# Quantized experts: tokens in tiles of four, the shared gate in halves, and two of three roundings on GpSimd

## The chip, the cores and the metric

The kernel runs on one core of one Trainium2 chip. A core has five engines that work side by side, each through its own instructions in a fixed order: TensorE (PE in the profile; PEld is its weight load), VectorE (DVE), ScalarE (ACT), GpSimd (POOL) and SyncE (SP), which here only issues DMAs. An instruction waits at the head of its engine's order until the semaphores that it names have been raised, and everything behind it on that engine waits with it. The metric is the time of one execution on the device in microseconds (us), less being better; the median of three runs is given, and one further execution was recorded by the profiler.

## The reference

The whole program is two decoder layers with six sublayers, each followed by a residual sum and a layer norm. The change lies in the first sublayer, a mixture of experts with quantized ("bit") linear layers. Cut to what matters:

```python
def bitlinear(x, w):
    xn = rmsnorm(x, BIT_EPS)
    xq = activation_quant(xn)      # round(x * 127 / max|x|), then scaled back
    wq = weight_quant(w)           # clip(round(w / mean|w|), -1, 1) * mean|w|
    return xq @ wq.T

def bit_mlp(x, gate_proj_w, down_proj_w):
    gate, y = split(bitlinear(x, gate_proj_w), 2)
    return bitlinear(silu(gate) * y, down_proj_w)
```

Each of 2048 tokens (16 blocks of 128, 256 numbers per token) goes through one shared expert and through the best two of eight routed experts, each of which takes 320 tokens at most. An expert's gate matrix is 256 x 1024 and its down matrix 512 x 256. To quantize a matrix one needs the mean of the absolute values of all of it; to quantize a token, or a row of the inner layer, one needs that row's largest absolute value and its sum of squares.

## The kernel before, in words

The sublayer is the function stage0 (L119 to L729). The order of every engine's work is written out by hand: no scheduler moves anything, and the order of the calls in the source is the order on each engine.

SP first issues the loads (L156 to L172): eight blocks of tokens as eight DMAs, the shared expert's gate (1 MB) and down matrix (0.5 MB), the other eight blocks, small tables, the transposed tokens xT for the router, the first routed expert's matrices, the context and more.

The head (L589 to L628) prepares the shared expert. For each block of tokens, squared (L266) sums squares on ACT, measured (L263) finds the largest value on DVE, steps (L273) makes the scale and quantized (L282) rounds the block with two DVE instructions; normed (L277) has POOL make the block's factor. For the weights, sum_down (L225) and sum_gate (L231) add up absolute values, total (L233) adds over the partitions with a matmul by ones on PE, means (L237) makes the scale, up (L242) scales and rounds on ACT by adding a large constant, and low and high (L246, L249) take the constant off again and clip, on DVE.

Then follows a loop of 36 turns (L689 to L729), one for each tile of 128 rows: 14 tiles of the shared expert, 20 of the routed experts, and two more shared ones. The turns overlap. In turn n, in the order of the source: ACT turns the earlier tile's transposed rows into bf16 (turned, L550); DVE multiplies the two halves of the inner layer (hidden, L516); ACT computes silu for the tile after (L511); DVE finds the row maximum (largest, L524), ACT the squares (L520), DVE the step and its reciprocal (step_of, L529 and L530) and the rounded inner rows m_r (rounded, L541); DVE (or ACT) scales the result of tile n-2 (done, L564 to L570); PE computes a bank of keys or values for a later stage (L1945, L1952), the gate of tile n+2 (gated, L503) and the down product of tile n-1 (down, L557); POOL makes the factor of tile n-1 (factor, L535: m_rt, m_rs, m_s); DVE or ACT copies the bank out (out_of, L585; from turn 11 on DVE does it in two turns of three, and not where n leaves 1 when divided by 3). Then come the jobs listed for the turn: quantizing the weights of the next routed experts (made_in, L636: the last DVE instructions of an expert fall in turns where n leaves 1), the router (logits L296, turn_logits L306, routes L314), copies of factors (backs_of, L454) and gathers of token rows by indirect DMA (fetch, L444) on POOL. Last, PE transposes the rounded rows (turn, L546).

The PSUM tile that down writes has one buffer, so down(n-1) waits until done(n-2) has read it. The tiles that the transposes write have two buffers, which the router's transposed logits share: while routes has not read those (L321), a later transpose waits.

After the loop the next stage begins with the gather of the routed results.

## Time and profile before

| what | value |
|---|---|
| median of three runs | 1404.76 us (1403.98 to 1405.64) |
| profiled execution | 1408.86 us, span from first to last instruction 1407.2 us |
| busy over the span | PE 88%, DVE 59%, ACT 48%, POOL 35% |
| mean granted TensorE clock | 0.954 of full speed |
| first tile: hidden(0) starts | 23.58 us |
| hidden(3), hidden(4), hidden(5) start | 39.71, 51.02, 58.64 us |
| last tile: hidden(35) starts | 191.35 us |
| first matmul of the next stage | 199.13 us |

The share of a whole span says little about a stage, so the sublayer has to be read in stretches of its own. A row of the table of stretches gives the length of the stretch, then for PE, PEld, DVE, ACT and POOL the busy time in us and the number of instructions, then the granted clock, the share of time in which the DMA engines moved data, and GB/s. A row of the timeline gives start, length, engine, line, operation, what is written and read with shapes, and in brackets how long the engine had been idle before and what released it. A row of the chain of waits gives start and length of a piece of the chain that ended last.

### The profile page before, as it was taken

Reading aid. Unit: us, or ns where it says so; the run is one execution under the profiler, and the core shown is the slowest. Engines: PE = TensorE matmul, PEld = TensorE weight load, DVE = VectorE, ACT = ScalarE, POOL = GpSimd, SP = SyncE. Lnnn points to the kernel's source line nnn. Section 1 sums busy time; section 2 is a strip of 40 time slices with the busy share of each in tenths; the row PEclk is TensorE's granted clock in tenths of the full one; section 3 lists DMA queues with packets and bytes.
Section 4 is the critical chain, followed back from the end, with each engine's and each line's share of the span. In section 5 each row is a group of like instructions: output and inputs, shape, how many; then the busy total and the mean of one; then the engine's idle time right before and its main releaser. Section 6 shows DMA issues by size and latency. Waiting matters only on the chain.

```text
span 1407.2 us, 19229 instructions
## 1 busy us (share of the span) xinstructions
PE 1234.8 (88%) x6731; PEld 843.2 (60%) x6743; DVE 824.7 (59%) x1755; ACT 676.4 (48%) x1733; POOL 495.5 (35%) x669
## 2 busy tenths in 40 slices
PE   4678887889978899866998999999889999999995
PEld 1455444666654566643655788877777655666553
DVE  7799968989957887856244565667333111211115
ACT  5779865778956665544223566654522111111110
POOL 4256547668861776640043233222202000000003
PEclk9899989989999999987899999999999999999998
DMA  8358324110011211100100222211005222232002
GB/s 311 131 174 295 114 79 85 17 39 31 32 50 60 74 51 46 53 16 24 52 0 1 73 78 62 75 61 45 1 8 187 71 98 68 78 105 96 17 8 75
DMA packets 63120, 103.53 MB, mean 74 GB/s; under 512 B 11920, under 2 KB 41712, under 8 KB 62768
## 3 DMA queue, kind: packets, MB, share of 16 engines
q1 hardware_dynamic: 60848, 96.76, 20.6%
q0 software_dynamic: 2176, 5.55, 1.9%
q8 instruction: 53, 0.87, 0.3%
q14 instruction: 43, 0.35, 0.1%
HBM read 81.74 MB, written 16.35 MB: 70 GB/s over the span
## 4 chain that ended last, share of the span: by engine, by line
PE 52%; DVE 29%; ACT 8%; POOL 6%; issue 4%; DMA 1%; another core or an unknown queue 0%; SPq 0%; DVEq 0%; ACTq 0%; POOLq 0%
PE ps_y L2453 7%; PE ps_m L2442 7%; PE ps_g L2442 7%; PE ps_m L1998 4%; DVE acc L1306 2%; PE ps_m L2129 2%; ACT s L2100 2%; PE ps_t L2120 2%; PE ps_m L2018 2%; DVE cT L1315 1%; DVE s L915 1%; DVE m L2094 1%; DVE s L2090 1%; PE ps_t L2109 1%; PE ps_s L2087 1%
## 5 line engine op out<-in xcount | busy, mean ns | idle before, releaser
L82 POOL TENSOR_SCALAR ln_t<-ln_mv 128x1 f32<-128x1 f32 (+1 forms) x84 | 16.6, 197 | 450.7 <-DVE ln_mv L90 309.1
L2447 DVE TENSOR_TENSOR h<-h,ps_m 128x512 f32<-128x512 f32 x60 | 41.3, 688 | 228.3 <-PE ps_m L2442 228.3
L2100 ACT ACTIVATE s<-s,m 128x128 f32<-128x128 f32 x256 | 99.4, 390 | 69.1 <-DVE m L2094 69.1
L2446 ACT ACTIVATE h<-ps_g 128x512 f32<-128x512 f32 x60 | 35.8, 597 | 171.0 <-PE ps_g L2442 171.0
L2442 PE MATMUL ps_g<-xin,w 128*128 128x512 f32 x224 | 106.3, 592 | 0.0
L2442 PE MATMUL ps_m<-xin,w 128*128 128x512 f32 x224 | 105.3, 592 | 0.0
L2453 PE MATMUL ps_y<-w,h 128*128 128x256 f32 x448 | 97.8, 379 | 0.0
L2453 PEld LDWEIGHTS ps_y<-w,h 128*128 128x128 f32 x448 | 85.1, 190 | 14.6 <-issue 3.3
L2104 POOL TENSOR_TENSOR s<-s,t 128x1024 f32<-128x1024 f32 x32 | 60.7, 1898 | 90.7 <-DVE t L2103 90.7
L927 ACT ACTIVATE s<-s,m 128x128 f32<-128x128 f32 x256 | 83.3, 395 | 11.7 <-DVE m L922 11.7
L2442 PEld LDWEIGHTS ps_m<-xin,w 128*128 128x128 f32 x224 | 42.5, 190 | 51.4 <-issue 50.2
L2442 PEld LDWEIGHTS ps_g<-xin,w 128*128 128x128 f32 x224 | 42.0, 190 | 46.4 <-issue 45.0
L1998 PE MATMUL ps_m<-xT,half 128*128 128x256 f32 x256 | 62.6, 389 | 2.6 <-DVE qT L2003 1.9
L2454 ACT COPY y<-ps_y 128x256 f32<-128x256 f32 x30 | 11.2, 372 | 104.7 <-PE ps_y L2453 67.7
L2090 DVE TENSOR_TENSOR s<-ps_s,hide 128x1024 f32<-128x1024 f32 x32 | 39.2, 1224 | 35.9 <-PE ps_s L2087 35.9
L2129 PE MATMUL ps_m<-half,oT 128*128 128x256 f32 x256 | 59.3, 385 | 0.0
L1306 DVE SCALAR_TENSOR_TENSOR acc<-ps_m,l1a_conv_w,acc 128x508 f32<-128x508 f32 (+2 forms) x72 | 53.3, 740 | 3.5 <-ACT acc L1299 1.8
L1998 PEld LDWEIGHTS ps_m<-xT,half 128*128 128x128 f32 x256 | 47.4, 194 | 9.2 <-DVE qT L2003 2.3
L2129 PEld LDWEIGHTS ps_m<-half,oT 128*128 128x128 f32 x256 | 47.4, 190 | 7.5
L83 POOL TENSOR_TENSOR ln_rs<-ln_t,mhalf 128x1 f32<-128x1 f32 (+1 forms) x84 | 48.7, 579 | 7.0
L2100 ACT ACTIVATION_READ_ACCUMULATOR s<-s,m 128x1 f32 x256 | 48.2, 188 | 0.0
L1414 POOL TENSOR_TENSOR mT<-mT,bc 128x1024 f32<-128x1024 f32 x16 | 37.8, 2360 | 28.4 <-ACT mT L1396 16.3
(524 smaller groups left out, 3102.1 us busy)
## 6 DMA issues: line engine op xcount, KB each, us to landing
w<-in_w_gate_dram SPq DMA_DIRECT2D x9, 1024.0 KB
csb<-cs_dram SPq DMA_DIRECT2D x16, 512.0 KB
w<-in_l1f_gateT_dram SPq DMA_DIRECT2D x14, 512.0 KB
w<-in_l1f_upT_dram SPq DMA_DIRECT2D x14, 512.0 KB
w<-in_l1f_downT_dram SPq DMA_DIRECT2D x14, 512.0 KB
k<-kv SPq DMA_DIRECT2D x20, 256.0 KB
v<-kv SPq DMA_DIRECT2D x20, 256.0 KB
ring<-k SPq DMA_DIRECT2D x10, 512.0 KB
```

Of the source, the lines that this page charges most:

```text
L83: return self.nc.gpsimd.tensor_tensor(out, t, self.mhalf[: out.shape[0], :n], ALU.pow)
L927: nc.scalar.activation(at, at, AF.Exp, bias=m[h][:, i:i + 1])
L1306: nc.vector.scalar_tensor_tensor(accv[:, :, j:], pcv[:, :, :P - j], w.conv[:, c, TAPS - 1 - j:TAPS - j], accv[:, :, j:], ALU.mult, ALU.add,)
L1414: nc.gpsimd.tensor_tensor(st[n].mT, st[n].mT, bc, ALU.mult)
L1998: nc.tensor.matmul(pq[:, j, :], wt[k][:, at], src[:, k, :], start=(k == 0), stop=(k == KD - 1))
L2090: nc.vector.tensor_tensor(half(b, j), pss.rearrange("p r c k -> p (r c) k"), hide.unsqueeze(1).to_broadcast([P, 8, P]), ALU.add,)
L2100: nc.scalar.activation(at, at, AF.Exp, bias=m[j][:, i:i + 1], accum_out=t[j][:, i:i + 1])
L2104: nc.gpsimd.tensor_tensor(half(b, j), half(b, j), t[j].unsqueeze(2).to_broadcast([P, 8, P]), ALU.mult)
L2129: nc.tensor.matmul(py[b], oT[b][:, c, :], w.o[c // 4][:, c % 4, :], start=(c == 0), stop=(c == NC - 1))
L2442: nc.tensor.matmul(ps[:, j, :], m[k][:, c * P:(c + 1) * P], self.r.xin[:, k, e, cols], start=(k == 0), stop=(k == KD - 1),)
L2447: nc.vector.tensor_tensor(h, h, pu, ALU.mult)
L2453: nc.tensor.matmul(pd, rows(c), w.down[c // 4][:, c % 4, :], start=(c == 0), stop=(c == FI // P - 1))
```

## The change

1. Loads. The tokens lie in four tiles of four blocks and come in four DMAs in place of sixteen. The shared gate comes in two halves of 0.5 MB right behind the first four blocks; the down matrix comes behind the second four.
2. The head. The shared expert has its own function, first_weights. Of the gate's absolute sums, ACT does one half and DVE the other; the gate is scaled, rounded and clipped half by half; the down matrix follows on its own, with a matmul for its mean of its own. Blocks 8 to 11 are measured, and blocks 12 to 15 squared, in turn 0; the quantizing of blocks 8 to 11 moves one turn later, and blocks 12 to 15 are all quantized in turn 3. POOL's factor for the router (rs_gate) is made in turn 1 in place of turn 0.
3. The loop. In turns where n does not leave 0 when divided by 3 (24 of 36), rounded runs on POOL. It stands in POOL's order ahead of the factor of tile n-1 and of the turn's jobs.
4. The gathers: two to a turn in place of three.

Behind the loop the order on every engine is as it was.

```diff
-        self.x = [self.new(self.const, [P, D], F32, f"x{b}") for b in range(NB)]
+        self.xs = [self.new(self.const, [P, 4, D], F32, f"x{g}") for g in range(NB // 4)]
+        self.x = [self.xs[b // 4][:, b % 4, :] for b in range(NB)]
...
-        for b in range(NB // 2):
-            nc.sync.dma_start(x[b], K.ins["x"][b])
-        load(NE)
-        for b in range(NB // 2, NB):
-            nc.sync.dma_start(x[b], K.ins["x"][b])
+        def load_tokens(g):
+            nc.sync.dma_start(K.xs[g], K.ins["x"][4 * g:4 * g + 4].rearrange("b p d -> p b d"))
+
+        load_tokens(0)
+        w = raw[NE] = K.new(wp, [P, 3, 4 * D], F32, "w")
+        for k in range(KD):
+            nc.sync.dma_start(w[:, k, :], K.ins["w_gate"][NE][k * P:(k + 1) * P, :])
+        load_tokens(1)
+        nc.sync.dma_start(
+            w[:, 2, :].rearrange("p (k n) -> p k n", n=D), K.ins["w_down"][NE].rearrange("(k p) n -> p k n", p=P),
+        )
+        load_tokens(2)
+        load_tokens(3)
...
+        def first_weights():
...
+            def sums():
+                nc.scalar.activation(q[:, 0, :], w[:, 0, :], AF.Abs, accum_out=acc[:, 0:1])
+                nc.vector.tensor_reduce(acc[:, 1:2], w[:, 1, :], AX.X, ALU.add, apply_absolute_value=True)
+
+            def mean(i):
+                pt = K.new(ps, [P, 1], F32, "ps_o", bufs=1)
+                at = (0, 1) if i == 0 else (2,)
+                for j in at:
+                    nc.tensor.matmul(pt, K.ones, acc[:, j:j + 1], start=(j == at[0]), stop=(j == at[-1]))
+                nc.vector.tensor_scalar(
+                    back[:, i:i + 1], pt, 1.0 / (D * 2 * FF) if i == 0 else 1.0 / (D * FF), 1e-5, ALU.mult, ALU.max,
+                )
+                nc.vector.reciprocal(s[:, i:i + 1], back[:, i:i + 1])
+
+            def up(k):
+                nc.scalar.activation(w[:, k, :], w[:, k, :], AF.Identity, scale=s[:, k // KD:k // KD + 1], bias=magic)
+
+            def whole(k):
+                to = q[:, k, :] if k < KD else qd[:, 0, :]
+                nc.vector.tensor_scalar(to, w[:, k, :], MAGIC, 1.0, ALU.subtract, ALU.min)
+                nc.vector.tensor_scalar(to, to, -1.0, None, ALU.max)
+
+            def sum_down():
+                nc.vector.tensor_reduce(acc[:, 2:3], w[:, 2, :], AX.X, ALU.add, apply_absolute_value=True)
...
         def rounded(n):
             g, t = tiles[n]
             r[n] = K.new(work, [P, FF], F32, "m_r", bufs=2)
-            nc.vector.tensor_scalar(r[n], h[n], g.s2[:, t:t + 1], MAGIC, ALU.mult, ALU.add)
+            on = nc.gpsimd if n % 3 else nc.vector
+            on.tensor_scalar(r[n], h[n], g.s2[:, t:t + 1], MAGIC, ALU.mult, ALU.add)
...
+        w = first_weights()
+        for b in range(2):
             quantized(b)
         normed(0)
-        w = weights(NE)
+        w.sums()
+        quantized(2)
+        w.mean(0)
+        quantized(3)
+        w.up(0)
         prepare(groups[0])
         tokens(groups[0], 0)()
+        w.whole(0)
+        scaled(groups[0])
+        w.up(1)
+        w.whole(1)
+        for b in range(4, 8):
+            squared(b)
+        w.sum_down()
+        gated(0)
+        silu(0)
+        w.mean(1)
+        w.up(2)
+        gated(1)
         for b in range(4, 8):
             measured(b)
+        w.whole(2)
         steps(1)
         normed(1)
...
+        for b in range(8, 12):
+            job(0, measured, b)
+        job(0, steps, 2)
+        job(0, normed, 2)
+        for b in range(12, 16):
+            job(0, squared, b)
+        job(1, lambda: K.rsqrt(small, rs_gate, ss, 1.0 / D, 1e-6, "rs_t"))
...
-            job((b - 8) // 2, quantized, b)
+            job(1 + (b - 8) // 2, quantized, b)
...
-            job(2 + (b - 12) // 2, quantized, b)
+            job(3, quantized, b)
...
-                job(m + t // 3, fetch, j, range(t, t + 1))
+                job(m + t // 2, fetch, j, range(t, t + 1))
```

## The prediction, made blind

> **What bounds the kernel now.** I read the stretches first. Behind the routed experts nothing changes, so only the first 199.1 us matter.
>
> ```profile
> core 0: us, PE busy (x) PEld busy (x) DVE busy (x) ACT busy (x) POOL busy (x), PEclk, DMA share, GB/s
> 58.64:100.00 41.36, 31.72 (x200) 22.77 (x203) 38.20 (x101) 32.60 (x52) 19.85 (x34) 0.96 0.41 132
> 100.00:140.00 40.00, 34.07 (x197) 23.49 (x200) 37.60 (x83) 35.78 (x59) 24.71 (x53) 1.00 0.87 283
> 140.00:163.30 23.30, 20.08 (x107) 10.67 (x105) 22.12 (x52) 20.21 (x32) 14.72 (x30) 1.00 0.39 132
> 163.30:183.60 20.30, 19.49 (x108) 10.77 (x109) 18.91 (x42) 13.38 (x27) 7.30 (x17) 1.00 0.31 114
> ```
>
> DVE is 92 to 95% busy from turn 5 (58.64) to 163.3; ACT follows with up to 89%. From 163.3 on PE is 96% busy. The chain of waits says the same: one DVE piece after another in the middle, PE at the end.
>
> ```profile
> 106.90 0.67 DVE m_h L516
> 107.59 0.70 DVE m_am L524
> 109.10 0.48 DVE x L564
> 109.58 0.60 DVE kv L585
> 110.18 1.12 DVE w_acc L225
> ...
> 176.42 1.72 PE ps_k L1952 x4
> ```
>
> So DVE time taken out of turns 5 to 26 shortens the run, and out of turns 27 to 33 it does not. The timeline shows how much goes with one rounding:
>
> ```profile
> 108.50 0.17 DVE L530 RECIPROCAL m_s<-m_st 128x1 f32<-128x1 f32 x1
> 108.70 0.49 DVE L541 TENSOR_SCALAR m_r<-m_h,m_s 128x512 f32<-128x512 f32 x1
> 109.10 0.48 DVE L564 SCALAR_TENSOR_TENSOR x<-ps_o,m_s,x 128x256 f32<-128x256 f32 x1
> ```
>
> The row is 0.49 long, but the next starts 0.40 after it: a rounding occupies DVE for 0.40.
>
> The early turns are bound by single waits:
>
> ```profile
> 13.24 1.22 DVE L225 TENSOR_REDUCE w_acc<-w 128x1 f32<-128x1024 f32 x1 [2.31 <-DMA w<-in_w_down_dram]
> ...
> 25.31 2.90 POOL L83 TENSOR_TENSOR rs_gate<-rs_t,mhalf 128x16 f32<-128x16 f32 x1
> ...
> 36.80 0.66 PE L546 MATMUL ps_t<-ident,m_r 128*128 128x128 f32 x4 [2.03 <-DVE pr L321]
> ...
> 39.71 0.75 DVE L516 SCALAR_TENSOR_TENSOR m_h<-ps_y,m_s,m_sg 128x512 f32<-128x512 f32 x1 [2.24 <-ACT m_sg L511]
> ```
>
> DVE waits for the shared weights; turn(1) waits until the router's logits are read (pr, 36.46), and hidden(3) hangs on that through turned(1), the tokens' copy and silu(3).
>
> The groups give prices, and a late stage shows what two engines do to each other:
>
> ```profile
> L541 DVE TENSOR_SCALAR m_r<-m_h,m_s 128x512 f32<-128x512 f32 x36 | 17.7, 492 | 1.8
> L1614 POOL TENSOR_SCALAR l1a_out_proj<-l1a_out_proj,l1a_ssm_norm_w 128x256 f32<-128x256 f32 x4 | 1.9, 484 | 0.0
> ```
>
> ```profile
> 402.28 0.73 POOL L989 TENSOR_TENSOR r<-x,bo_all 128x256 f32<-128x256 f32 x1
> 402.35 0.81 DVE L1003 TENSOR_SCALAR x<-r,ln_mv,ln_rs 128x256 f32<-128x256 f32 x1 [0.36 <-POOL ln_rs L83]
> ```
>
> L1003 takes 0.40 where POOL is idle (386.16). Here it lasts until 0.15 after POOL's end: DVE was held, and of its own 0.40 it had 0.25 behind it. The reductions (L524) and the reads of PSUM (L564, L585) show no such stretching.
>
> **The change, part by part.** *Loads.* Tokens land now 0.66 apart ((5.44 - 2.80)/4, blocks 0 to 4); SP stalls on them from 5.55 to 13.56. In one DMA four blocks land at 2.80 + 0.39 MB at 199 to 373 GB/s (slowest and fastest early rate), so 3.9 to 4.8: I take 4.3, against 4.7 for the fourth block now. Each 0.5 MB behind it takes 1.4 at 373 GB/s: gate halves 5.7 and 7.1, blocks 4 to 7 8.5, down 9.9, where now the gate lands at 11.74 and down at 13.24. SP's remaining loads start some 4 us earlier; none is waited for in the loop. Seven DMAs in place of eighteen save SP issue time that nothing waits for later; the store of the quantized tokens (turn 3) goes out 1.2 later, its first gather is in turn 8.
>
> *Head.* DVE in its new order: measured 0 to 3, 1.5 (5.8); steps (6.2); two blocks quantized, 0.6 each (7.4); half the gate summed 1.22 (8.65); identity cast and third block (9.5); mean (9.9); fourth block (10.5). ACT's up(0) takes 1.25 (L244, half size) to 11.2, whole(0) 0.69 + 0.43 to 12.4. ACT copies xqT (1.0) before up(1), so whole(1) ends at 14.6; down's sum 15.9; PE's gate matmuls hold its mean back to 16.85; measured 4 to 7 18.3; whole(2), behind silu's table load and up(2), 19.8; steps and four blocks 22.6. hidden(0) then starts at 22.6 instead of 23.58: -1.0, and not the 4 us by which the weights come sooner, because DVE took on half the gate's sum (+1.22) and now waits for ACT in small pieces. Measuring blocks 8 to 11 (1.4 + 0.4) falls to turn 0 and quantizing two (1.2) leaves it: hidden(1) at 27.05 (-0.3).
>
> *Turns 1 to 4.* Turn 1 without its rounding: hidden(2) -0.6. POOL's queue then holds m_r(1), the factor of tile 0 (1.25), rs_gate (0.2 + 2.9) and only then normed(3) and m_r(2). rs_gate ends at about 35.4, where it ended at 28.2; L321 now waits for it and starts at 35.55, against 36.46: hidden(3) -0.9. The four quantized blocks in turn 3 fill DVE's wait for the router's exp (1.1 now). m_r(2) comes at 38, still ahead of its transpose (41.67 - 0.9). In turn 4 the rounding's 0.40 goes: hidden(5) -1.3. If rs_gate comes 0.9 later, this falls to -0.4; if the tokens land at 3.9 it is -1.7.
>
> *Rounding on POOL.* No row has POOL on this form. L82 with one element takes 0.19, L1614 with 256 0.484; straight on, 512 elements give 0.77. Upper end: two-input POOL rows of 512 elements, 1.28 (L935). I take 0.77: same operation, one input. DVE to POOL takes 0.14 (22.69 to 22.83). With the reciprocal's end as zero, POOL works from 0.14 to 0.91, while DVE runs done from 0.03 to 0.46. Next on DVE:
> - n leaves 2 from turn 8 on (8, 11, 14, 17, 20, 23, 26): a PSUM read or copy, then a reduction. Nothing is held; -0.40 each, -2.8.
> - n leaves 1 (7, 10 to 25 by threes) and turn 5: L247 or L390, operations of the held kind (a two-input one: L750 takes 3.82 for two of 0.48 at 270.06, beside POOL's sums). By the row above they end 0.91 - 0.25 after zero plus their length, 0.20 later than free: -0.20 each, eight times -1.6.
>
> Turns 1 and 2 hold nothing: in 1 DVE's quantizing is first, in 2 POOL comes late. m_r is ready for PE at 0.97, when down(n-1) (now released 0.40 sooner by done) ends: turn(n) is not late. Behind m_r on POOL waits the factor of tile n-1, ready at 2.2; done(n-1) needs it a turn (4.2) later. In the last turns PE transposes at 195.61 what was rounded by 193.80; 0.4 more is hidden there.
>
> *POOL's queue.* After turns 13, 19 and 25 it is: m_r 0.77, factor 1.25, eight copies of 0.22, two gathers of 1.12 (one in 25) and gaps 0.3: 6.3 (5.1) against turns of 4.2 to 4.6. The next m_r comes 1.7 (0.6) late, turn(n) 1.3 (0.2) later than now; PE's waits for done of 0.5 to 1.0 hide about half: +1.5. Spreading the gathers costs nothing else: POOL idles 63 us waiting for squares.
>
> *ACT and PE close behind* (89%, 86%) take back a tenth of 4.4: +0.4. From 163.3 on 0: PE bounds.
>
> Sum: -1.3 - 2.8 - 1.6 + 1.5 + 0.4 = -3.8. The profiled execution, 1408.86 with span 1407.2 and 1.66 around it, becomes 1405.1; it lies 4.1 above the median 1404.76, so in the median's terms 1401.0.
>
> The Trainium skill, SBUF — State Buffer, section Who interferes with whom, speaks against the change: DVE's two-port and two-input operations and GpSimd exclude each other, and "the other fully blocks" for the whole instruction. The rows above agree that it blocks, but credit 0.25 already done. Without that credit the eight held turns would gain nothing (0.45 of waiting against 0.40), and the sum would be -1.8.
>
> **The rivals.** *Slower: POOL's rounding is dear.* If 512 elements with two operations cost 1.5, the eight held turns lose 1.5 - 0.57 - 0.40 = 0.53 each (+4.2), the free ones keep 0.2 (-1.4), the head keeps -0.3, POOL's queue costs 1.5: 1408.8. It decides above about 1.35. For it: 1.28 for two inputs; against: L1614.
>
> *Nothing measurable: other waits take it.* rs_gate late by 0.9 (-0.4 in the head), ACT and PE take half of 4.4, queue +0.3: about -1.5, 1403.3. For it: ACT's 89% at 100 to 140, and the chain's excursions to PE at 82 to 89, 114 and 141.
>
> *Much faster: no holding.* All fifteen turns give 0.40 (-6.0), head -2.0 with early tokens: -8, 1396.8. For it: weights four us sooner; against: L1003.
>
> **How the numbers follow.** Chances: forecast 0.40, no change 0.24, much faster 0.20, slower 0.16. A measurement here tells about 0.2%, 2.8 us. The forecast's own range is 1398.5 to 1403, so a quarter of it counts as same; of the no-change case a sixth as faster; of the slower case nearly all as slower. Faster 0.54, same 0.31, slower 0.15. The range reaches through most of the outer cases: 1395.5 to 1408.5.
>
> **What the profile after would show.** Right: m_r on POOL at about 0.77; hidden(0) near 22.6 and hidden(5) near 57.3; L247 stretched by 0.2 or more in turns that leave 1; the next stage's first matmul near 195.3. Wrong: m_r above 1.3, POOL's waits ending in long DVE runs with turn(n) waiting for m_r, or hidden(0) below 21, which would mean that DVE did not bound the head.

## The result, and the profile after

The changed kernel takes 1406.63 us (median of 12 runs; without one of them, which took 2089.76 us at a granted clock of 0.554 and is left out of the ratio, the median is 1405.45 and the range 1402.59 to 1414.17); the kernel before took 1405.31 us (12 runs beside them, 1400.49 to 1410.56). The ratio is 1.0008, with a 95% interval of 0.9990 to 1.0026: no difference that can be told. The profiled execution took 1414.17 us (span 1412.3, mean granted clock 0.947), 5.3 more than the profiled execution of before.

Line numbers of the changed kernel are higher: hidden is L559, the row maximum L567, the step and reciprocal L572 and L573, the rounding L585, POOL's factor L83, L84 and L579, the transposes L590, done L608 and L614, the copied bank L629, the weights' low and high L255 and L258, gathers L492, copies of scales L503 to L506.

The stretches of the profile after, from hidden(5) on, with cuts at 100 and 140 as before, at hidden(27) and at hidden(33) (columns as there):

```profile
core 0: us, PE busy (x) PEld busy (x) DVE busy (x) ACT busy (x) POOL busy (x), PEclk, DMA share, GB/s
56.50:100.00 43.50, 33.40 (x209) 23.87 (x210) 40.25 (x101) 35.09 (x57) 23.97 (x42) 0.92 0.45 145
100.00:140.00 40.00, 33.30 (x193) 22.54 (x196) 36.13 (x76) 34.27 (x54) 30.23 (x58) 1.00 0.88 281
140.00:161.30 21.30, 18.89 (x100) 10.13 (x98) 19.58 (x44) 19.16 (x32) 15.18 (x30) 1.00 0.31 104
161.30:184.65 23.35, 20.80 (x115) 11.14 (x114) 17.63 (x40) 15.21 (x31) 12.71 (x27) 1.00 0.30 105
```

DVE has fallen from 94 to 90% between 100 and 140 and from 95 to 92% behind it. The last row should not be set against the 96% of before, whose cuts lay elsewhere: from hidden(27) to hidden(33) PE was busy for 19.79 of 21.81 us before, 91%, against 89% now. Work has left DVE, but the tiles don't come faster by as much: somebody waits. What the roundings cost on POOL, and who waited for them, stands in the view of the tile m_r:

```profile
L585 POOL TENSOR_SCALAR m_r<-m_h,m_s x24: 677/687/1672, 28.8 to 192.0; 128x512 f32<-128x512 f32 x24
...
who waited for it (us, times):
  ACT m_hT L594: 27.9, 21
  PEld ps_t L590: 9.8, 7
  PE ps_t L590: 8.0, 6
```

The rounding takes 0.69 in the median (shortest, median, longest in ns), but up to 1.67, and PE sat 8.0 us waiting for it, where before it never did. Since each turn starts with its hidden(n) on DVE, the starts of hidden(n) tell where time went. The table adds up by how much the turns differ from the first profile of before (negative: shorter; turn n runs from hidden(n) to hidden(n+1)):

| turns | forecast | after |
|---|---|---|
| up to hidden(5) | -1.3 | -2.14 |
| 8, 11, ... 26 (n leaves 2) | -2.8 | -3.31 |
| 7, 10, ... 25 (n leaves 1), with turn 5 | -1.6 | +1.31 |
| behind POOL's queue: 21 and 27 | +1.5 | +1.71 and +1.48 |
| all others up to hidden(28) | | -0.08 |
| hidden(28) | | -1.03 |
| hidden(28) to hidden(35) | 0 | -0.41 |
| hidden(35) to the next stage's first matmul | 0 | +0.47 |
| sum: next stage's first matmul | -3.8, with +0.4 for ACT and PE | -0.97 (198.16) |

### The profile page after: what moved, and what is told of

Its sections match the earlier page's. It is cut to its first block, busy times and chain, and to the rows that moved or that the text cites. A ratio compares the mean times of both kernels' runs of the same rounds, so it can differ in the third digit from the quotient of the medians.

```text
span 1412.3 us, 19212 instructions
## 1 busy us (share of the span) xinstructions
PE 1245.6 (88%) x6735; PEld 851.8 (60%) x6747; DVE 823.9 (58%) x1735; ACT 674.7 (48%) x1734; POOL 512.1 (36%) x693
## 4 chain that ended last, share of the span: by engine, by line
PE 54%; DVE 23%; ACT 8%; POOL 8%; issue 4%; DMA 2%; another core or an unknown queue 0%; SPq 0%; POOLq 0%; DVEq 0%; ACTq 0%
PE ps_y L2501 7%; PE ps_m L2490 7%; PE ps_g L2490 7%; PE ps_m L2046 4%; ACT s L2148 2%; DVE acc L1354 2%; PE ps_t L2168 2%; PE ps_m L2177 2%; PE ps_m L2066 2%; DVE m L2142 1%; DVE s L2138 1%; DVE cT L1363 1%; DVE s L963 1%; PE ps_s L956 1%; PE ps_t L998 1%
## 5 line engine op out<-in xcount | busy, mean ns | idle before, releaser
L83 POOL TENSOR_SCALAR ln_t<-ln_mv 128x1 f32<-128x1 f32 (+1 forms) x84 | 16.3, 194 | 457.7 <-DVE ln_mv L91 308.5
L84 POOL TENSOR_TENSOR ln_rs<-ln_t,mhalf 128x1 f32<-128x1 f32 (+1 forms) x84 | 48.5, 577 | 7.0
```

The costliest lines, as they stand in the source:

```text
L84: return self.nc.gpsimd.tensor_tensor(out, t, self.mhalf[: out.shape[0], :n], ALU.pow)
```

## The experiments

In the diffs here "-" is the changed kernel unless another is named. A free turn is one where n leaves 2, a held turn one where n leaves 1. "Next stage" is the start of the next stage's first matmul, the end of the sublayer that the change touches.

**The kernel before, profiled again.** No edit.

> The kernel before, unchanged, profiled once more, to see how far hidden(n) moves with nothing changed. In the kernel with the old head and roundings on GpSimd hidden(0) came at 22.89 against 23.58 in the first profile, with the same code up to there. Theory A (the weights' landing scatters): hidden(0) between 22.6 and 23.6, the turns from 5 to 14 and 16 to 34 as long as in the first profile to within 0.1, turn 15 and the stretch from hidden(35) to the next stage's first matmul off by up to 1.5. Rival (the stage repeats to within 0.2 everywhere): hidden(0) at 23.6 and the next stage at 199.1.

hidden(0) came at 22.57 in place of 23.58, hidden(5) at 58.06 (-0.58), turn 15 was 0.51 shorter, the last stretch 0.56 shorter, the next stage began at 197.63 in place of 199.13. All turns from 8 to 14 and 16 to 34 were the same within 0.03. Theory A. So with the order of work unchanged a turn's length can be compared to a few hundredths (turn 7, which moved by 0.18, and turn 15 excepted), but the head, turn 15 and the last stretch move by half a microsecond to one without any change; and the whole execution took 1397.53 us, 11.3 less than the first profiled one.

**The head alone.**

```diff
-            on = nc.gpsimd if n % 3 else nc.vector
+            on = nc.vector
```

> The changed kernel with all 36 roundings back on VectorE; the loads, the split shared weights, the turns 0 to 4 and the gathers' places stay as changed. Theory A (the head gives about 2, the roundings on GpSimd give nothing in sum): hidden(5) starts 1.7 before the 58.64 of the kernel before (2.14 in the changed kernel, less the 0.4 of turn 4's rounding), the turns from 6 to 26 take what they took before to within 0.1, and the next stage's first matmul is at 197.6 (199.13 before, 198.16 changed). Theory B (whatever VectorE gains early is taken back by ScalarE and TensorE before the stage ends): next stage at 198.8 to 199.2. Total: A about 1.5 us below before (ratio 0.999), B 1.000.

hidden(5) at 57.70: 0.94 before the first profile, 0.36 before the second. From turn 6 on the turns took what they took before within 0.24, but for turn 15 (-1.21). Next stage 196.53, ratio 0.9976 (0.9959 to 0.9993). Theory A for what follows the head, though with up to 0.24 in place of its 0.1; but the head gave half of what A said, and turn 15 and the last stretch (-0.88), two of the places that scatter, brought the next stage forward instead. Of the changed kernel's 2.14, 1.33 fall in turn 4, which is as long as before here, with its rounding back on DVE.

**The roundings alone**, on the kernel before:

```diff
-            nc.vector.tensor_scalar(r[n], h[n], g.s2[:, t:t + 1], MAGIC, ALU.mult, ALU.add)
+            on = nc.gpsimd if n % 3 else nc.vector
+            on.tensor_scalar(r[n], h[n], g.s2[:, t:t + 1], MAGIC, ALU.mult, ALU.add)
...
-                job(m + t // 3, fetch, j, range(t, t + 1))
+                job(m + t // 2, fetch, j, range(t, t + 1))
```

> The kernel before with only the roundings of two turns in three moved to GpSimd and the gathers two to a turn; loads and head as before. Theory A: turns that leave 2 are 0.4 to 0.5 shorter each, turns that leave 1 are 0.2 longer each, turns 21 and 27 are 1.5 to 1.7 longer because the rounding of turn 20 and 26 stands behind copies and gathers in GpSimd's queue; next stage at 199.9 to 200.5, total ratio 1.0005 to 1.001. Rival (the prediction's prices: -0.2 in each turn that leaves 1 and +1.5 for the queue in all): next stage at 196.3.

The turns behave as in the changed kernel: those that leave 2 give -3.05, those that leave 1 cost +1.42, turns 21 and 27 cost +1.71 and +1.48, just as there. hidden(28) is 0.19 before the first profile and 0.75 behind the second. The next stage, at 196.83, was not as late as A said, because the last stretch took 1.7 less, one of the places that scatter. Ratio 0.9977 (0.9966 to 0.9987). So within the turns more is lost from turn 7 on than the free turns give; A's total is not borne out, and the rival's 196.3, though near in the sum, is wrong in each of its terms.

**A third of the roundings, in free turns.**

```diff
-            on = nc.gpsimd if n % 3 else nc.vector
+            on = nc.gpsimd if n % 3 == 2 else nc.vector
```

> The changed kernel with GpSimd rounding only in the turns that leave 2 (12 of 36), where VectorE has no two-port run behind its reciprocal. Theory A (the loss sits in the turns that leave 1): each of the turns 8, 11, 14, 17, 23 gives 0.45, the turns that leave 1 are as long as before, turns 20 and 26 still lose 0.7 to 1 behind copies and gathers; hidden(28) 3 before the old one, next stage at 196.0 to 197.0, total ratio 0.998. Rival (the loss sits in GpSimd's queue alone): next stage at 198, as in the changed kernel.

The turns that leave 2 gave -3.43; those that leave 1 cost 0.67 where the changed kernel lost 1.38, nearly all of it in turn 7 (0.19, which scatters) and in turn 22 (0.43, of which more below); turn 21 cost 0.04. But turn 27 cost 4.49, turn 15 1.03, and the next stage came at 200.09; ratio 0.9987 (0.9966 to 1.0009). The timeline shows what happened to the rounding of turn 26:

```profile
161.61 0.18 POOL L506 COPY m_b<-w_back 64x1 f32<-64x1 f32 x1 [1.55 <-issue]
...
162.81 1.06 POOL L492 DMA_INDIRECT xe<-xq_dram,token  x1 [0.29 <-POOL m_b L506]
...
163.97 0.70 POOL L585 TENSOR_SCALAR m_r<-m_h,m_s 128x512 f32<-128x512 f32 x1
164.72 1.05 PE L590 MATMUL ps_t<-ident,m_r 128*128 128x128 f32 x4 [2.56 <-POOL m_r L585]
```

POOL stood still for 1.55 among the copies for no reason that the trace names; the copies and a gather stood ahead of the rounding; PE waited 2.56 for it, and its four transposes then took 1.05, where those of the turn ahead took 0.60. The granted clock from 158 to 171 was 0.87 (1.00 in the kernel with the head alone). Theory A is right on the turns that leave 2 and on those that leave 1 but for turn 22; turn 27 it undercounted.

**A third of the roundings, in held turns.**

```diff
-            on = nc.gpsimd if n % 3 else nc.vector
+            on = nc.gpsimd if n % 3 == 1 else nc.vector
```

> The changed kernel with GpSimd rounding only in the turns that leave 1 (12 of 36), where the low and high halves of the expert's weights follow on VectorE. Theory A: each of the turns 7 to 25 that leave 1 ends 0.2 to 0.3 later than with all on VectorE, GpSimd's rounding takes 1.0 to 1.7 there, hidden(27) at about 0 to -0.5 against before, next stage at 198.6 to 199.3, total ratio 1.000. Rival (the prediction's -0.2 for each such turn): next stage at 196.2 and ratio 0.998.

The turns that leave 1 are 1.01 longer in sum, 0.8 more than with the head alone; hidden(27) is 1.14 before the first profile, so 0.6 later than with the head alone; POOL's rounding took 1.24 to 1.73 in five of seven such turns. But turn 22 alone is 1.04 longer, and that ahead of its reciprocal, where DVE waited 1.51 for PE (0.35 before). Turn 16 cost 0.31, turn 10 0.11, and turns 7, 13, 19 and 25 are 0.10 to 0.12 shorter each. The next stage, 196.85, and the ratio, 0.9976 (0.9960 to 0.9991), are better than A said: the head, turn 15 (-1.22) and the last stretch (-0.74) were short. Neither A's loss of 0.2 to 0.3 in each such turn is there nor the rival's gain of 0.2: a held turn gives about 0.1 or loses up to 0.3.

**Where the time of a held turn goes.** The trace of the changed kernel has both orders of arrival. The timeline of DVE and POOL in turns 13 and 19:

```profile
101.54 0.17 DVE L573 RECIPROCAL m_s<-m_st 128x1 f32<-128x1 f32 x1
101.62 0.47 DVE L608 SCALAR_TENSOR_TENSOR x<-ps_o,m_s,x 128x256 f32<-128x256 f32 x1
101.87 0.69 POOL L585 TENSOR_SCALAR m_r<-m_h,m_s 128x512 f32<-128x512 f32 x1 [5.27 <-DVE m_s L573]
102.00 1.10 DVE L255 TENSOR_SCALAR q_d<-w 128x1024 bf16<-128x1024 f32 x1
...
128.41 0.67 DVE L255 TENSOR_SCALAR q_d<-w 128x1024 bf16<-128x1024 f32 x1
128.68 1.49 POOL L585 TENSOR_SCALAR m_r<-m_h,m_s 128x512 f32<-128x512 f32 x1 [1.46 <-DVE m_s L573]
129.00 0.69 DVE L258 TENSOR_SCALAR q<-q 128x2048 bf16<-128x2048 bf16 x1
129.61 0.84 DVE L258 TENSOR_SCALAR q_d<-q_d 128x1024 bf16<-128x1024 bf16 x1
```

In turn 13 POOL began first: its rounding takes 0.69 and DVE's L255 1.10 where it takes 0.68 with POOL idle. In turn 19 DVE began first: POOL's rounding takes 1.49, through two DVE runs, and the third run on DVE, L258 on q_d, takes 0.84 where it takes 0.42 alone. Either way DVE loses 0.42. What has left it is worth a little more: L255 starts 0.46 after the start of the reciprocal in turn 13, where it started 0.99 after it before. So these turns are 0.11 to 0.12 shorter from the reciprocal on. In the second case the rounding is late as well, by 0.8.

The sum of +1.31 must then lie elsewhere. The table splits the eight turns of the changed kernel at the start of the reciprocal (differences from the first profile of before), and gives how long after it POOL began to round:

| turn | 5 | 7 | 10 | 13 | 16 | 19 | 22 | 25 | sum |
|---|---|---|---|---|---|---|---|---|---|
| up to the reciprocal | 0.00 | -0.01 | +0.22 | +0.27 | 0.00 | 0.00 | +0.75 | 0.00 | +1.23 |
| from the reciprocal on | -0.07 | -0.11 | +0.17 | -0.12 | +0.31 | -0.11 | -0.12 | +0.13 | +0.08 |
| POOL begins to round after | 0.33 | 0.34 | 1.00 | 0.33 | 0.80 | 0.35 | 0.33 | 1.44 | |

The second row says that held turns give and take nothing in sum. They lose where POOL begins late, and in turns 10, 16 and 25 it does because a gather stands in its queue straight ahead of the rounding, as in turn 16:

```profile
115.19 1.06 POOL L492 DMA_INDIRECT xe<-xq_dram,token  x1 [0.16 <-issue]
116.30 1.23 POOL L585 TENSOR_SCALAR m_r<-m_h,m_s 128x512 f32<-128x512 f32 x1
```

Two other kernels had the same gather out of the way in time. In the one with its queue cleared (below), whose turn 15 was longer, the rounding of turn 16 begins 0.34 after the reciprocal, and the stretch is 0.11 shorter than before in place of 0.31 longer; in the one with roundings in held turns only the same holds for turn 25 (0.34, and 0.10 shorter in place of 0.13 longer). The first row is a wait that comes ahead of any rounding of its turn: DVE needs PE's sum for the weights' mean, and PE's matmul for it waits until ACT has turned the tile ahead. Turns 10 and 22, first before, then in the changed kernel:

```profile
89.17 0.16 DVE L238 TENSOR_TENSOR w_back<-ps_t,parts 128x2 f32<-128x2 f32 x1 [0.72 <-PE ps_t L235]
143.97 0.16 DVE L238 TENSOR_TENSOR w_back<-ps_t,parts 128x2 f32<-128x2 f32 x1 [0.35 <-PE ps_t L235]
```

```profile
86.47 0.16 DVE L246 TENSOR_TENSOR w_back<-ps_t,parts 128x2 f32<-128x2 f32 x1 [0.95 <-PE ps_t L243]
142.33 0.16 DVE L246 TENSOR_TENSOR w_back<-ps_t,parts 128x2 f32<-128x2 f32 x1 [1.10 <-PE ps_t L243]
```

In the three kernels that round only in free turns and keep the gathers' places, turns 10 and 22 still lose 0.23 and 0.44 or 0.45 there, with nothing held; with the head alone they lose nothing. So part of what a free turn gives is handed back at the next such wait for PE and ACT. The rest of turn 22's 0.75 was not taken apart; in the changed kernel it follows the late transposes of turn 21.

**A rounding that nobody waits for.** On the kernel with the head alone:

```diff
             on = nc.vector
+            if n > 4 and n % 3:
+                nc.gpsimd.tensor_scalar(K.new(work, [P, FF], F32, "m_no", bufs=1), h[n], g.s2[:, t:t + 1], MAGIC, ALU.mult, ALU.add)
```

> The head alone, all roundings on VectorE, and beside them GpSimd rounds the same rows once more, from turn 5 on in two turns of three, into a tile that nobody reads: its price to VectorE alone, without anyone who waits for its result. Theory A (each engine holds the other): in turns that leave 2 GpSimd's rounding takes 0.69 and the turn is as long as with the head alone, within 0.1; in turns that leave 1 VectorE's two-port run on the weights gets 0.2 to 0.6 longer, the turn too, and GpSimd's rounding takes 1.0 to 1.7. Rival (VectorE goes first and only GpSimd is held): the turns that leave 1 are as long as with the head alone, within 0.1, and what the changed kernel loses there is TensorE's wait for the late rounding.

The timeline of DVE and POOL in turn 10:

```profile
90.77 0.48 DVE L587 TENSOR_SCALAR m_r<-m_h,m_s 128x512 f32<-128x512 f32 x1
91.17 0.48 DVE L610 SCALAR_TENSOR_TENSOR x<-ps_o,m_s,x 128x256 f32<-128x256 f32 x1
91.47 0.70 POOL L586 TENSOR_SCALAR m_no<-m_h,m_s 128x512 f32<-128x512 f32 x1
91.56 1.15 DVE L255 TENSOR_SCALAR q_d<-w 128x1024 bf16<-128x1024 f32 x1
```

L255 takes 1.15 with a rounding beside it that no instruction reads, and 0.68 in the same turn with the head alone; the turn is 0.27 longer than in the first profile of before (0.47 longer than with the head alone). Turns 13 and 25, where the idle rounding mostly ran beside DVE's own, are 0.09 and 0.10 longer. Theory A: DVE itself is held, where nobody waits for POOL's result. Of the turns that leave 2 the turns 8, 11, 14, 20 and 26 are as long as with the head alone within 0.05, but 17 and 23 cost 1.58 and 0.84, as turns 16 and 22 ahead of them cost 0.90 and 2.11. The waits of PE between 85 and 160 us name a cause:

```profile
PE ps_t L515 <- DMA xe<-xq_dram,token: 1.7, 3, 0.8
```

The idle roundings pushed POOL's gathers back until PE waited for the gathered rows. Turn 22 has one of these waits (0.82), and the granted clock between 145 and 158 us was 0.74. In turns 8, 11, 17 and 23 the idle rounding took 0.91 to 0.98, not 0.69: it ran beside DVE's own rounding. In turns 14, 20 and 26 it came later and took 0.69.

**The queue.** The chain of waits of the changed kernel, from turn 19 to turn 21:

```profile
128.68 1.49 POOL m_r L585
130.25 0.25 POOL m_rt L83
130.57 0.56 POOL m_rs L84
131.52 0.18 POOL m_b L503
...
133.19 1.06 POOL xe L492
134.25 0.30 issue
134.56 0.95 POOL xe L492
135.59 0.69 POOL m_r L585
136.33 0.66 PE ps_t L590 x4
```

The chain has left DVE: it goes through everything that POOL has ahead of the rounding of turn 20, which starts at 135.59, 3.4 after the reciprocal that it needs (132.04 and 0.16). PE's transposes had waited 2.44 for it. Three kernels move this queue. The first keeps all 24 roundings:

```diff
-            job(7 + 6 * j, backs_of, g)
+            job((7, 13, 21, 26)[j], backs_of, g)
             for t in range(5):
-                job(m + t // 2, fetch, j, range(t, t + 1))
+                m = (8, 13, 18, 23)[j] + ((0, 0, 1, 1, 2), (0, 0, 1, 1, 2), (0, 0, 0, 2, 2), (0, 0, 0, 1, 1))[j][t]
+                job(m, fetch, j, range(t, t + 1))
```

> The changed kernel with its 24 roundings on GpSimd, but the copies of scales that stood in turns 19 and 25 and the gathers of 19 and 25 put behind the roundings of 20, 21 or 26. Theory A (these alone made the roundings of 20 and 26 late): turn 21 loses 0.1 to -0.4 instead of 1.71, turn 27 nothing instead of 1.48; hidden(28) about 3.5 to 4 before the old one (changed kernel: 1.03), next stage at 195.5 to 196.5. Rival (the rounding of turns 19 and 25, stretched by VectorE to 1.0 to 1.5, makes the next one late by itself): turns 21 and 27 still lose 1 each, hidden(28) 1.5 before the old one.

Turn 21 costs 0.03 in place of 1.71 and turn 27 0.74 in place of 1.48, so copies and gathers did make those roundings late. They did so together with the stretched rounding of turn 19: where POOL rounds in free turns only, and copies and gathers stay, turn 21 costs 0.03 or 0.04 too. But turn 22 costs 1.57 and turn 23 0.96. The timeline has the reason for turn 22:

```profile
109.52 1.12 PE L590 MATMUL ps_t<-ident,m_r 128*128 128x128 f32 x4 [2.46 <-POOL m_r L585]
...
141.05 0.29 PE L515 MATMUL ps_t<-identb,xe 128*128 128x128 bf16 x2 [1.55 <-DMA xe<-xq_dram,token]
```

The last gather of the third group, moved behind the rounding of turn 20, now lands after PE wants its rows. The first line is the rounding of turn 14, where nothing was moved. The changed kernel has the same wait of 2.46 there, then transposes of 0.66, and loses nothing in turns 14 and 15; here they took 1.12, the granted clock between 105 and 112 us was 0.81 (1.00 there; 0.50 from 109.5 to 112), and turn 15 was 1.61 longer. Next stage 198.69, ratio 0.9996 (0.9980 to 1.0012): neither theory's number, since the gathers have a date of their own.

The second has only the roundings of the turns that leave 2, and moves copies and gathers behind them:

```diff
-            on = nc.gpsimd if n % 3 else nc.vector
+            on = nc.gpsimd if n % 3 == 2 else nc.vector
...
-            job(7 + 6 * j, backs_of, g)
-            for t in range(5):
-                job(m + t // 2, fetch, j, range(t, t + 1))
+            job(8 + 6 * j, backs_of, g)
+            for t, m in enumerate(((8, 8, 9, 9, 9), (12, 12, 14, 14, 15), (18, 18, 20, 20, 21), (21, 23, 23, 24, 24))[j]):
+                job(m, fetch, j, range(t, t + 1))
```

> GpSimd rounds only in the turns that leave 2, and the copies of the scales and the gathers stand behind such a rounding instead of ahead of it. Theory A: each of the turns 8 to 29 that leave 2 is 0.45 shorter, the turns that leave 1 are as long as before, and nothing is lost in turns 20, 21, 26 and 27; hidden(27) 4.0 to 4.8 before the old one and next stage at 195.5 to 196.5, total ratio 0.997. Rival (ScalarE, TensorE and the stores of the early keys take it back): hidden(27) less than 3 before the old one, next stage at 197 or later.

Turns 21 and 27 cost nothing, but turn 22 costs 4.01: two gathers land late there, and one each in turns 11 and 17, which cost 0.12 and 0.90 where they should have given 0.45. From the waits of PE between 85 and 160 us:

```profile
PE ps_t L515 <- DMA xe<-xq_dram,token: 4.5, 4, 1.8
```

Behind these waits the granted clock was 0.72 between 140 and 152 us. Next stage 199.63, ratio 1.0044 (1.0032 to 1.0056): slower as a whole, and a miss for A; the rival's times hold, for another reason than it gives. The gathers that I moved cost the sublayer its gain; the whole lost more than the sublayer did.

The third has as many roundings on POOL as the changed kernel, but in the turns that leave 2 and 0:

```diff
-            on = nc.gpsimd if n % 3 else nc.vector
+            on = nc.vector if n % 3 == (1 if n > 4 else 0) else nc.gpsimd
...
-            job(7 + 6 * j, backs_of, g)
-            for t in range(5):
-                job(m + t // 2, fetch, j, range(t, t + 1))
+            job(8 + 6 * j, backs_of, g)
+            for t, m in enumerate(((9, 9, 9, 9, 9), (12, 12, 12, 12, 15), (18, 18, 18, 18, 21), (21, 24, 24, 24, 24))[j]):
+                job(m, fetch, j, range(t, t + 1))
```

> From turn 5 on GpSimd rounds in the turns that leave 2 or 0 and VectorE in those that leave 1, where the two-port runs follow; copies and gathers stand in turns that leave 2 or ahead of VectorE's roundings. As many roundings on GpSimd as in the changed kernel. Theory A (what counts is what follows VectorE's reciprocal, not how many roundings move): GpSimd's rounding takes 0.69 in nearly all of them, the turns that leave 2 and those that leave 0 are 0.4 to 0.5 shorter each; hidden(27) 5 to 7 before the old one, next stage at 194 to 195.5, total ratio 0.996. Rival (ScalarE at 85 to 90% and TensorE bound the turn once VectorE has less): hidden(27) 3 to 4 before, as with a third of the roundings.

The view of the tile m_r, and the timeline of turn 11:

```profile
L585 POOL TENSOR_SCALAR m_r<-m_h,m_s x24: 687/687/797, 28.8 to 195.4; 128x512 f32<-128x512 f32 x24
```

```profile
94.84 0.48 DVE L608 SCALAR_TENSOR_TENSOR x<-ps_o,m_s,x 128x256 f32<-128x256 f32 x1 [1.82 <-POOL m_s L579]
95.38 0.60 PE L601 MATMUL ps_o<-q_d_s,m_hT 128*128 128x256 bf16 x4 [2.17 <-DVE x L608]
```

All 24 roundings take 0.69 to 0.80, against 0.68 to 1.67: theory A on what sets their price. But the gathers, put together four or five at a time, made POOL's factor late, and DVE's done waits 1.82 for it, PE 2.17. The turns that leave 2 cost 2.29 in sum where they should have given 3. Next stage 200.15, ratio 1.0042 (1.0024 to 1.0060). The times of A and of the rival both missed.

**A version with neither loss.** POOL rounds in the turns that leave 2, without turn 26; copies and gathers stay where the changed kernel has them.

```diff
-            on = nc.gpsimd if n % 3 else nc.vector
+            on = nc.gpsimd if n % 3 == 2 and n != 26 else nc.vector
```

> The changed kernel with GpSimd rounding only in the turns that leave 2, without turn 26, whose rounding stood behind copies and a gather; copies and gathers where the changed kernel has them. Theory A: the turns 8, 11, 14, 17, 20, 23, 29 are 0.45 shorter each, all others as long as before but for the scatter of turn 15 (up to 1.2 either way); hidden(28) 3.5 to 5 before the first profile of the kernel before and 2.5 to 4 before its second one, next stage at 195 to 196.5; total ratio 0.996 to 0.998. Rival (the stage gives nothing to fewer roundings, since gathers and stores set its end): hidden(28) less than 2 before the first profile, as with no rounding moved.

The turns that leave 2 give -2.97, each of the six before turn 26 its 0.43 to 0.54; those that leave 1 cost 0.47 (0.44 of it in turn 22); turns 21 and 27 0.06 together; turn 15 +0.56. hidden(28) is 2.40 before the first profile of before and 1.46 before the second, short of A's 3.5 and 2.5; next stage at 195.81, as A said. Ratio 0.9987 (0.9961 to 1.0014).

The same with a fourth buffer for the copied banks:

```diff
-            t = K.new(work, [P, 512], F32, "kv", bufs=3)
+            t = K.new(work, [P, 512], F32, "kv", bufs=4)
```

> As the run before it, with four buffers in place of three for the copied keys and values. Theory A (turn 15 sometimes waits for the store of an earlier copy: 2.15 of waiting in the kernel with the roundings of 12 free turns): turn 15 takes 4.4 to 4.6 in place of 4.4 to 6.7; next stage 0 to 1 earlier than without. Rival (turn 15 waits for TensorE, not for a buffer): turn 15 scatters as before.

Turn 15 took 4.42 in place of 6.19; hidden(28) is 3.96 before the first profile of before, 3.02 before the second; next stage at 194.28, 4.85 and 3.35 earlier than in the two profiles of before and 3.88 earlier than in the changed kernel. In the run before it DVE had waited 1.48 in that turn for the store of a bank, and 2.15 in the kernel with a third of the roundings; here it waited for none. Whether the buffer is needed is open all the same: the kernel with the head alone had a turn 15 of 4.42 with three buffers. The median is 1399.88 us against 1405.09, ratio 0.9975 (0.9958 to 0.9993): 0.25% faster than the kernel before. That ratio does not rank the versions, for the head alone, the roundings alone and the roundings in held turns have 0.9976 or 0.9977 too, with sublayers that end 2.3 to 2.6 us earlier than in the first profile of before; and the kernel before itself had medians from 1403.99 to 1406.74 beside the different experiments. From the waits of PE between 85 and 160 us, first of the changed kernel, then of this one:

```profile
PE ps_t L590 <- POOL m_r L585: 7.5, 5, 2.5
```

```profile
PE ps_t L590 <- POOL m_r L585: 1.0, 1, 1.0
```

**The loads alone**, on the kernel before: tokens in tiles of four and the shared gate in halves ahead of the second four blocks (the part of the change in L156 to L172), the head's order as before.

> The kernel before with the changed loads alone: tokens in tiles of four, the shared gate in halves ahead of the second four blocks, then down. Order of the work as before, so VectorE sums down alone, in one piece, and ScalarE sums the gate. Theory A (the weights come 3 to 4 us sooner, and VectorE's 2.3 of waiting for them goes, but the first four blocks are measured 1.5 later): hidden(0) at 21.5 to 22.2, earlier than 22.1 to 22.6 of the changed head; hidden(5) about 57.0 to 57.5. Rival (the order of the head was needed to use the loads): hidden(0) at 23.0 or later.

hidden(0) at 24.57, later than in either profile of before: the rival. The timeline of DVE, then that of ACT:

```profile
5.09 1.40 DVE L273 TENSOR_REDUCE am<-x 128x1 f32<-128x256 f32 x4 [3.36 <-DMA x<-in_x_dram]
...
10.18 0.35 DVE L293 TENSOR_SCALAR m_q<-x,sc 128x256 f32<-128x256 f32 x1 [3.16 <-ACT m_q L277]
```

```profile
9.24 0.42 ACT L277 ACTIVATE m_q<-x 128x256 f32<-128x256 f32 x1 [2.45 <-DMA x<-in_x_dram]
```

DVE's wait for the weights has gone, but in the old order ACT squares eight blocks first, and the second four now land at 9.24, together and behind the gate; DVE's first quantizing waits for that. The whole is no faster, ratio 1.0011 (0.9991 to 1.0031). The reordered head was needed to use the loads.

## Why the prediction was right or wrong

The time, 1406.63, lies in the range of 1395.5 to 1408.5, and "within 0.2%" had a chance of 0.31; but the forecast was 1401.0, faster by 0.27%, and the interval of the ratio, from 0.9990 on, leaves that out. "Faster", the likeliest outcome at 0.54, did not come, and that the time still lies in the range is owed to the width of the range. By its steps:

*Loads.* Wrong by about 1 us: the first four blocks landed at 5.25 where I had taken 4.3 (4.7 to 5.4 in the other kernels).

*Head.* hidden(0) at 22.60 is the number forecast, hidden(3) at 38.92 stands against 38.8, and L364 (L321 before) started at 35.66 against 35.55. hidden(5) at 56.50 came 0.8 earlier than forecast, by turn 4, which gave 1.33 in place of 0.40. Yet the reading of "-1.0" was lucky: the kernel before has hidden(0) anywhere between 22.57 and 23.58. The head alone gave 0.4 to 0.9 at hidden(5).

*The rounding's price on POOL.* Forecast 0.77, measured 0.69 where nothing interferes. The rival of a dear rounding, 1.35 and more, holds in some held turns only (1.49, 1.50, 1.67 in the changed kernel), and for another reason than its own length.

*Turns that leave 2.* Forecast -2.8, measured -3.31: right, each 0.40 to 0.54.

*Turns that leave 1: the step that failed.* "By the row above they end 0.91 - 0.25 after zero plus their length, 0.20 later than free: -0.20 each, eight times -1.6." Measured +1.31, in two parts.

From the reciprocal on, the stretch that the term is about, the eight turns gave +0.08 in sum. The credit of 0.25 for work already done was taken from L1003, an operation of 256 elements; L255 in turn 13 started at 102.00, POOL ended at 102.56, and L255 ended 0.54 after that, so of its 0.68 it had 0.14 behind it. It would also have been free earlier than I had put it, 0.29 after the reciprocal's end and not 0.46. So where POOL begins at once the turn gives 0.11 or 0.12 (turn 5 only 0.07) and not 0.20, whichever engine begins first. And POOL does not always begin at once: "Spreading the gathers costs nothing else" was wrong, since a gather ahead of the rounding in turns 10, 16 and 25 made it late, and these turns lost 0.13 to 0.31.

The other +1.23 stands ahead of the reciprocal in turns 10, 13 and 22, where DVE, now earlier, waits for PE's sum for the weights' mean. The term had nothing for it.

The Trainium skill, SBUF — State Buffer, section Who interferes with whom, says both: that whoever issues first keeps the shared ports for the whole instruction, and that the other waits it out. The prediction set the rule against L1003 and sided with the row; the rule's -1.8 for the sum, which it gave beside, was the better number, as the +0.08 of the held stretches shows. What the page does not say, and the lines of turn 19 show, is that the loser waited through two runs that followed each other.

*POOL's queue.* "+1.5" was too small: turn 21 alone lost 1.71 and turn 27 1.48, while behind turn 13, the third place named, turns 14 and 15 lost nothing: PE waited 2.46 for its rounding, and DVE's next tile was not held up. The rounding of turn 20 came 3.4 after its reciprocal, since the one of turn 19, stretched to 1.49, stood in the same queue ahead of the copies and gathers. PE's waits for done, which were to hide half, hid little: it waited 2.44 for the transposes' input. The kernel that moved copies and gathers away got turn 21's loss back, so the place was right and the size was not.

*ACT and PE close behind, +0.4.* Right in kind, and too small. In the kernel with the fourth buffer every free turn gives its full 0.42 to 0.58, but turns 10 and 22 hand back 0.23 and 0.45 in DVE's wait for PE. In the changed kernel such waits are 1.23, some of it POOL's doing.

*The last part, 0.* Nearly: -0.41 to hidden(35), and +0.47 in a stretch that moved by 0.56 with nothing changed.

*The sum.* -3.8 forecast; -0.97 measured against the first profile of before and +0.53 against the second. The rival "other waits take it" had -1.5, near in size, and in part in kind: it blamed ACT, PE and a late rs_gate. The takers were the ports that DVE and POOL hold against each other, with the gathers ahead of three roundings (1.7 of the forecast gone), POOL's queue in turns 21 and 27 (another 1.7) and DVE's waits for PE (1.2, where 0.4 had been set down); the early turns, the free turns and the rest gave back 1.4. The first two are shown by the turns' lengths, by the durations of L255, L258 and L585, and by the kernel that rounds in free turns only, without turn 26; the third is read from the traces, and no run removes it alone.

*From the profiled execution to the median.* Taking 4.1 off, the distance of the first profiled execution from the median, was sound, but the second profiled execution lies 7.2 below that median. Behind the sublayer nothing is changed, and still the profiled execution of the changed kernel lost 6.4 between 244 and 260 us (drift -0.56 ahead, +5.85 behind), and the second profile of the kernel before gained 9.8 behind the sublayer. One instruction's row of the timeline of before, and the rows of after at the same place:

```profile
257.07 1.44 DVE L764 TENSOR_SCALAR x<-x,ln_mv,ln_rs 128x256 f32<-128x256 f32 x4
```

```profile
258.20 6.16 DVE L812 TENSOR_SCALAR x<-x,ln_mv,ln_rs 128x256 f32<-128x256 f32 x4
...
258.90 0.84 POOL L1037 TENSOR_TENSOR r<-x,bo_all 128x256 f32<-128x256 f32 x1
259.72 2.34 POOL L983 TENSOR_TENSOR sum<-s 128x1024 f32<-128x1024 f32 x1
262.13 2.08 POOL L983 TENSOR_TENSOR sum<-sum 128x512 f32<-128x512 f32 x2
```

Four operations that take 1.44 together took 6.16 and ended just behind POOL's sums (264.21): in that execution the two met, in four others (the second profile of before, the head alone, the free turns with the queue cleared, the fourth buffer) they take 1.44 or 1.45. DVE was late there: it had just waited 2.68 for PE, whose granted clock was 0.50 from 247 to 251 us (0.69 in the first profile of before). What remains open is whether the start of the later stages sets such meetings and clocks: the kernels with roundings in the turns 2 and 0, and with the cleared queue and free turns, are 0.4% slower as a whole, more than the 0.5 to 2.5 us by which their sublayer ends later than in the two profiles of before.

## What to carry to other kernels

Before moving work from DVE to POOL, look at what DVE runs next to it: where a run of the held kind follows within the length of the moved instruction, DVE loses nearly all that it was spared (0.42 of 0.53 here), and more than that if the moved instruction comes late; the turns without such a run give the full 0.40 to 0.54. Then read the engine's queue as a list of dates, with every copy and gather ahead of the moved instruction and every gather behind it, because an engine that is a third busy can still be late for both. And split a turn at the place that was changed before blaming the change: most of what the held turns lost stood ahead of it. Compare lengths of turns rather than ends of executions: here most turns repeat to 0.03 us, and the whole execution only to about ten.

## What the runs showed of the hardware

- DVE and POOL held each other in both directions: L255 1.10 for 0.68, L258 0.84 for 0.42, and POOL's rounding 1.49 for 0.69 through two DVE runs in a row. An idle rounding of POOL beside DVE's own rounding took 0.91 to 0.99, while DVE's stayed at 0.49 in the median and 0.55 at most.
- After PE had waited some 2.5 us, the four transposes that followed took 1.05 and 1.12 in two of these kernels, and 0.66 in the changed one after the same wait; where gathers came late the granted clock of the stretch fell to 0.72. A late rounding or gather can cost more than its own lateness.
- Profiled executions of one and the same kernel were 11.3 us apart, 9.8 of them in stages behind this one.
